# Graph network, three projections: the next tile's rows turned ahead of this tile's products, and the v's turned one tile later

## The chip, the cores and the metric

The kernel runs on one core of a Trainium2 chip. The metric is the device time of one execution in microseconds (us), the median of several runs. Engines are called by their names in the profile: PE is TensorE (matrix products and transposes; PEld is its loading of weights), DVE is VectorE, ACT is ScalarE, POOL is GpSimd, and SP is the engine that issues most transfers.

## The reference, cut to what matters

A graph of 2708 nodes with 512 features passes four layers, each of the form x = layernorm(x + layer(x, adj)). The first two average neighbours; the third is graph attention with 8 heads of 64; the fourth is graph attention with 8 heads, a second attention with one head of 512, and a small MLP. The change lies in the projections of the attentions:

```python
Wh = jnp.einsum('ni,hio->hno', h, W)              # the projection
f1 = jnp.einsum('hno,ho->hn', Wh, a1)             # per target row
f2 = jnp.einsum('hno,ho->hn', Wh, a2)             # per source row
e = leaky_relu(f1[:, :, None] + f2[:, None, :], 0.2)
attention = softmax(where(adj > 0, e, -9e15), axis=-1)
h_prime = jnp.einsum('hnm,hmo->hno', attention, Wh)
```

The projection is made three times: for layer 2 (8 heads), for the first attention of layer 3 (8 heads), and for its second attention (one head; called the output layer here). Between the last two an elu is applied.

## The kernel before, in words

The 2708 rows are cut into 22 tiles, 21 of 128 rows and one of 20. `project` (L502) makes one projection; it is called at L892 for layers 2 and 3 and at L897 for the output layer. For each tile t it does the following.

- The rows of the tile come from DRAM. `source` says how: `plain` (L758) only loads them; `summed` (L761) loads the attention's output `rows` and the old features `spare`, adds them (L764), normalises (`layer_norm`, L106: bn_stats L108, L110, L112, a power on POOL L113, L114) and stores the result to `x3_dram` (L766); `elu_first` (L769) loads and applies an elu (L753 to L756, its exponential on ACT). The tile `rows` has three buffers, `spare` two.
- `transposed` (L116) turns the rows: four transposes on PE into the PSUM tile `ps_tr` (L120), then one copy on ACT to `xT` (L122). Both have two buffers. The helper `early` (L145) makes results once and some tiles ahead: the rows one tile ahead of the turning (L521), the turned rows when they are asked for (L522).
- Eight products (L529) accumulate over four slices of 128 features into two PSUM tiles, `pm0` and `pm1`, of two buffers each: 256 columns of Wh each, and behind them the columns for f1 (in `pm0`) or f2 (in `pm1`). The profile counts each product twice, as two passes.
- From `pm`, DVE copies the f2 part to `dcol` (L534) and the clamped f1 part to `b` (L536, two buffers). ACT makes exponentials of them (`ecol` L538, `ucol` L539, `vcol` L549), and Wh is scaled into `R2` (on DVE, L543, with heads; on ACT, L547, without). The profile writes `R` for R2.
- `b` is turned on PE into `ps_v` (L556), and ACT writes its exponential into a row of `vrow` (L557). Where a block of target tiles is complete, `vrow` is sent to `v_dram` (L560). There are two blocks of 11 tiles in layers 2 and 3, and six of up to 4 tiles in the output layer. At the end of a block in layers 2 and 3, DVE also splits factors into bf16 parts (L563 to L568, `split` L493).

The attention follows. Each head and block loads its row of `v_dram` over all partitions (`v_bc`, L592). For each source tile, DVE makes the weights `e` (L598, four buffers), ACT a mask `c` of them by a sigmoid (L606), and PE multiplies `e` with R2 (L734). The output layer's attention multiplies at L857 and then runs the MLP (L823, L832).

What sets the order of the work: the program is written as one stream, and the framework's scheduler orders each engine's instructions from it by the dependences and by its own estimate of times. It may move an instruction before others that stand ahead of it in the source, so attention work of the first block (`e`, `c`) comes to stand among the later tiles of a projection. The order on each engine is then fixed, and each engine waits in it for the semaphores of the others. Transfers that SP issues (`rows`, `spare`, `v_dram`, `v_bc`) share one such queue. In the projection no order is written out by hand.

Of the kernel before, what the change touches and what calls it, by code (L numbers as in the profile page):

```python
# [9 lines left out]
F32 = mybir.dt.float32  # L10
# [3 lines left out]
AF = mybir.ActivationFunctionType  # L14
# [4 lines left out]
P = 128  # L19
# [3 lines left out]
ALPHA = 0.2  # L23
# [7 lines left out]
def kernel(  # L31
# [9 lines left out]
    nc = tc.nc  # L41
    N = x.shape[0]
    NT = -(-N // P)
    FULL = N // P
    H, HO = l2_w.shape[0], l2_w.shape[2]
# [4 lines left out]
    def rows(t):  # L50
        return min(P, N - t * P)
# [9 lines left out]
    ident = const.tile([P, P], F32, name="ident")  # L61
# [54 lines left out]
    def transposed(pool, psum, src, n, name, order=as_it_comes):  # L116

        ps = psum.tile([P, KD, P], F32, name="ps_tr")
        for k in range(KD):
            order(nc.tensor.transpose(ps[:, k, :n], src[:, k * P:(k + 1) * P], ident[:n, :n]))  # L120
        dst = pool.tile([P, KD, P], F32, name=name)
        nc.scalar.copy(dst[:, :, :n], ps[:, :, :n])  # L122
        return dst
# [15 lines left out]
    def weight_tile():  # L139
        return ahead.tile([P, KD, 2, D // 2 + H], F32, name="w", bufs=1)  # L140
# [4 lines left out]
    def early(first, n, make):  # L145

        made = {}

        def get(i, **how):
            for j in range(len(made), min(i + first + 1, n)):  # L150
                made[j] = make(j, **how)
            return made[i]
        return get
# [36 lines left out]
    with ExitStack() as phase:  # L190
# [16 lines left out]
        sm = phase.enter_context(tc.tile_pool(name="l01", bufs=2))  # L207
# [19 lines left out]
        with ExitStack() as ph:  # L227
# [36 lines left out]
            xTs = early(0, NT, lambda t, order=as_it_comes: transposed(ahead, ps_tr, xs(t), rows(t), "xT", order))  # L264
# [11 lines left out]
            for t in range(NT):  # L276
                n = rows(t)
# [25 lines left out]
        with ExitStack() as ph:  # L303
            st = ph.enter_context(tc.tile_pool(name="l0b", bufs=1))
            b_nb = bias(bcast(l0_b_nb, D))
            cuts = [(b, min(b + 4, NT)) for b in range(0, NT, 4)]
            cuts = cuts[-1:] + cuts[:-1]
# [87 lines left out]
            for i, b in enumerate(cuts):  # L395
                ts_ = range(*b)
                cols, w = slice(b[0] * P, b[1] * P), (b[1] - b[0]) * P
# [17 lines left out]
                for t in ts_:  # L415
                    n = rows(t)
# [8 lines left out]
            xTs = early(0, NT, lambda t: transposed(ahead, ps_tr, xs(t), rows(t), "xT"))  # L425
            for t in range(NT):
                n = rows(t)
# [9 lines left out]
        with ExitStack() as ph:  # L437
            st = ph.enter_context(tc.tile_pool(name="l1b", bufs=2))
            for t in range(NT):
                n = rows(t)  # L440
# [52 lines left out]
    def split(pool, dst, src):  # L493

        rest = pool.tile([P, NT, H], F32, name="rest", bufs=1)[:, :src.shape[1], :src.shape[2]]
        nc.vector.tensor_copy(dst[:, :, :, 0], src)
        nc.vector.tensor_sub(rest, src, dst[:, :, :, 0])
        nc.vector.tensor_copy(dst[:, :, :, 1], rest)
        nc.vector.tensor_sub(rest, rest, dst[:, :, :, 1])
        nc.vector.tensor_copy(dst[:, :, :, 2], rest)  # L500

    def project(name, source, layer, v_dram, cuts):  # L502


        w_src, w_view, _, heads = atts[layer]

        w = weight_tile()
        hh = max(heads // 2, 1)
        for k in range(KD):
            for a in range(2):  # L510
                src = (w_src[4 * a:4 * a + 4, k * P:(k + 1) * P, :].rearrange("h p o -> p h o") if heads > 1 else
                       w_src[k * P:(k + 1) * P, a * D // 2:(a + 1) * D // 2].rearrange("p (h o) -> p h o", h=1))
                nc.scalar.dma_start(w[:, k, a, :D // 2].rearrange("p (h o) -> p h o", h=hh), src)
        nc.gpsimd.tensor_copy(w[:, :, :, D // 2:D // 2 + heads], wa[:, layer, :, :, :heads])
        with ExitStack() as ph:
            sm = ph.enter_context(tc.tile_pool(name=f"{name}_s", bufs=2))
            ps_tr = ph.enter_context(tc.tile_pool(name=f"{name}_ptr", bufs=2, space=PSUM))
            ps_mm = ph.enter_context(tc.tile_pool(name=f"{name}_pmm", bufs=2, space=PSUM))
            ps_v = ph.enter_context(tc.tile_pool(name=f"{name}_pv", bufs=2, space=PSUM))
            width = max(z - a for a, z in cuts) * P  # L520
            xs = early(1, NT, lambda t: source(sm, t, rows(t)))  # L521
            xTs = early(0, NT, lambda t: transposed(ahead, ps_tr, xs(t), rows(t), "xT"))  # L522
            for t in range(NT):
                n = rows(t)
                xT = xTs(t)
                pm = [ps_mm.tile([P, D // 2 + H], F32, name=f"pm{a}") for a in range(2)]
                for k in range(KD):
                    for a in range(2):
                        nc.tensor.matmul(pm[a][:n, :D // 2 + heads], xT[:, k, :n], w[:, k, a, :D // 2 + heads],  # L529
                                         start=(k == 0), stop=(k == KD - 1))  # L530
                if t + 1 < NT:
                    xTs(t + 1)
                d = dcol[:n, t, :heads]
                nc.vector.tensor_copy(d, pm[1][:n, D // 2:D // 2 + heads])  # L534
                b = sm.tile([P, H], F32, name="b")
                nc.vector.tensor_scalar(b[:n, :heads], pm[0][:n, D // 2:D // 2 + heads], -RANGE, RANGE,  # L536
                                        op0=OP.max, op1=OP.min)
                nc.scalar.activation(ecol[:n, t, :heads], d, AF.Exp, scale=ALPHA)  # L538
                nc.scalar.activation(ucol[:n, t, :heads], d, AF.Exp, scale=1.0 - ALPHA)  # L539
                for a in range(2):  # L540
                    to, src = R2[:n, t, a * D // 2:(a + 1) * D // 2], pm[a][:n, :D // 2]
                    if heads > 1:
                        nc.vector.tensor_mul(to.rearrange("p (h o) -> p h o", h=hh),  # L543
                                             src.rearrange("p (h o) -> p h o", h=hh),
                                             ecol[:n, t, a * hh:(a + 1) * hh, None].to_broadcast([n, hh, HO]))
                    else:
                        nc.scalar.activation(to, src, AF.Copy, scale=ecol[:n, t, 0:1])  # L547
                if heads > 1:
                    nc.scalar.activation(vcol[:n, t, :], b[:n, :], AF.Exp, scale=ALPHA - 1.0)  # L549
                    nc.gpsimd.tensor_scalar(bcol[:n, t, :], ucol[:n, t, :], -STEP * (1.0 + 2.0 ** -22), None,  # L550
                                            op0=OP.mult)
                a, z = next(c for c in cuts if c[0] <= t < c[1])
                if t == a:
                    vrow = sm.tile([heads, width], F32, name="vrow", bufs=1)
                ps = ps_v.tile([P, P], F32, name="ps_v")
                nc.tensor.transpose(ps[:heads, :n], b[:n, :heads], ident[:n, :n])  # L556
                nc.scalar.activation(vrow[:, (t - a) * P:(t - a) * P + n], ps[:heads, :n], AF.Exp, scale=ALPHA - 1.0)  # L557
                if t == z - 1:
                    cols = slice(a * P, a * P + (z - 1 - a) * P + n)
                    nc.sync.dma_start(v_dram[:, cols], vrow[:, :cols.stop - cols.start])  # L560
                    if heads > 1:
                        ue = sm.tile([P, NT, H], F32, name="ue", bufs=1)[:, :z - a]
                        nc.vector.tensor_mul(ue, ucol[:, a:z], ecol[:, a:z])  # L563
                        split(sm, parts_m[:, a:z], ue)
                        for k in range(2):
                            nc.vector.tensor_scalar(pairs_c[:, a:z, :, k, 6 * k:6 * k + 3], parts_m[:, a:z, k::2, :],
                                                    -1.0, None, op0=OP.mult)
                            split(sm, pairs_c[:, a:z, :, k, 6 * k + 3:6 * k + 6], ecol[:, a:z, k::2])  # L568
            sq = sm.tile([P, NT, H], F32, name="sq", bufs=1)
            if heads < H:  # L570
                nc.vector.memset(sq, 0.0)
            dd = dcol[:, :, :heads]
            nc.vector.tensor_mul(sq[:, :, :heads], dd, dd)
            sq = sq.rearrange("p t h -> p (t h)")
            nc.vector.tensor_scalar(sq, sq, RANGE * RANGE, None, op0=OP.is_le, op1=OP.add,
                                    accum_out=okc[:, layer:layer + 1])
# [33 lines left out]
    cuts = [-((-NT * i) // nb) for i in range(nb + 1)]  # L610
# [278 lines left out]
    for i, (source, dst) in enumerate(((plain, o_dram[0]), (summed, o_dram[1]))):  # L889
        with ExitStack() as ph:  # L890
            att = Weights(ph, f"a{2 + i}", blocks, vd[i])
            project(f"p{2 + i}", source, i, vd[i], blocks)  # L892
            heads_attention(f"a{2 + i}", att, dst)
# [332 lines left out]
```

## Time and profile before

The time is 3125.3 us, the median of three runs (3123.17 to 3129.33). The profiled execution has a span of 3125.8 us at a mean granted TensorE clock of 0.996.

| Stretch (us from the span's start) | What runs there | PE busy | DVE busy | ACT busy |
|---|---|---|---|---|
| 925 to 1024 | projection of layer 2 | 92.84 of 99 | 35.91 | 40.63 |
| 1609 to 1718 | projection of layer 3 | 96.98 of 109 | 72.05 | 38.58 |
| 2305 to 2404 | projection of the output layer | 92.74 of 99 | 37.96 | 48.71 |
| all, 3125.8 | | 3009.5 | 1988.8 | 1401.3 |

How to read it: a stretch is a part of the one execution on the chip that the profile shows. Busy times count the instructions of an engine; matrix products are pipelined, so that a busy PE need not be at its peak. In a line of the timeline stand start, duration, engine, line of the source, operation, the tiles written and read, and in square brackets how long the engine was idle before and what it waited for. The projections take about a tenth of the span.

### The profile page before, as it was taken

The page shows a single profiled execution, that of the slowest core. Times are in us where ns is not written, and L with a number is a line of the kernel's source. Part 1 is how long each engine was busy: PE and PEld are TensorE (multiplying, and loading weights), DVE is VectorE, ACT ScalarE, POOL GpSimd, SP SyncE. Part 2 cuts the span into 40 slices and gives each one's busy share as a digit, 9 for nine tenths or more (in the row PEclk, how much of TensorE's full clock was granted, in tenths as well). Part 3 has the DMA queues.
Part 4 walks back from the last instruction along what each step waited for, and adds up shares of the span by engine and source line. Part 5 has one row for each costly group of instructions (what it writes and reads, how often), then busy time and mean ns, then how long its engine had stood idle before and what let it go on. Part 6 is the DMA issues. An engine that isn't in the chain of part 4 may idle for free.

```text
span 3125.8 us, 37086 instructions
## 1 busy us (share of the span) xinstructions
PE 3009.5 (96%) x14888; PEld 1647.0 (53%) x14888; DVE 1988.8 (64%) x2562; ACT 1401.3 (45%) x1575; POOL 223.2 (7%) x352
## 2 busy tenths in 40 slices
PE   8999999999999999999998999999999999999998
PEld 4556666448887433333356333333356455555555
DVE  5562765212233899999986999999963524345342
ACT  2431000112224688888863788899863000000011
POOL 2220010101110000000012000000000000000001
PEclk9999999999999999999999999999999999999999
DMA  5651421322222000110024010011021000000000
GB/s 137 139 127 35 121 64 41 108 65 81 81 70 76 15 29 35 39 44 30 28 80 145 22 39 28 27 38 33 20 97 48 4 14 17 24 14 22 14 19 21
DMA packets 114287, 163.31 MB, mean 52 GB/s; under 512 B 39494, under 2 KB 62311, under 8 KB 114104
## 3 DMA queue, kind: packets, MB, share of 16 engines
q1 hardware_dynamic: 88152, 109.21, 11.5%
q0 software_dynamic: 16064, 47.95, 5.6%
q10 hardware_dynamic: 9888, 3.67, 0.5%
q8 instruction: 119, 1.95, 0.3%
q14 instruction: 64, 0.52, 0.1%
HBM read 130.92 MB, written 44.55 MB: 56 GB/s over the span
## 4 chain that ended last, share of the span: by engine, by line
PE 65%; issue 19%; DVE 10%; ACT 2%; DMA 2%; POOL 1%; DVEq 0%; POOLq 0%; SPq 0%; ACTq 0%
PE pn L857 13%; PE pm L221 10%; PE po L734 9%; PE acc L450 7%; DVE e L598 6%; PE acc L408 5%; PE pm L529 5%; PE pl L832 5%; PE pl L823 5%; PE pd L665 2%; ACT c L606 1%; PE ps_tr L120 1%; PE acc L254 1%; DMA rows<-o_dram 1%; PE pm L401 1%
## 5 line engine op out<-in xcount | busy, mean ns | idle before, releaser
L598 DVE SCALAR_TENSOR_TENSOR e<-v_bc,ucol,maskT 128x1300 f32<-128x1300 f32 (+3 forms) x836 | 1187.4, 1473 | 345.6 <-PE pn L857 317.9
L606 ACT ACTIVATE c<-e,bcol 128x1300 fp8e4<-128x1300 f32 (+1 forms) x704 | 993.9, 1423 | 113.0 <-DVE e L598 61.7
L734 PE MATMUL po<-e,R 128*64 128x512 f32 (+2 forms) x4224 | 946.4, 550 | 47.4 <-DVE e L598 47.3
L734 PEld LDWEIGHTS po<-e,R 128*64 128x64 f32 x4224 | 340.5, 136 | 600.3 <-issue 384.9
L857 PE MATMUL pn<-e,R 128*128 128x512 f32 (+1 forms) x1056 | 413.5, 542 | 0.0
L857 PEld LDWEIGHTS pn<-e,R 128*128 128x128 f32 x1056 | 191.0, 190 | 199.4 <-issue 195.9
L529 PE MATMUL pm<-w,xT 128*128 128x264 f32 (+3 forms) x1056 | 247.7, 388 | 17.1 <-ACT xT L122 16.6
L529 PEld LDWEIGHTS pm<-w,xT 128*128 128x128 f32 (+1 forms) x1056 | 191.3, 187 | 58.5 <-ACT xT L122 24.4
L408 PE MATMUL acc<-yH,kT 128*128 128x512 f32 x484 | 214.0, 442 | 0.0
L825 ACT ACTIVATE w<-pl,b 128x256 f32<-128x256 f32 (+1 forms) x88 | 40.9, 465 | 372.9 <-PE pl L823 372.9
L450 PE MATMUL acc<-yH,mf 128*128 128x512 f32 x484 | 192.7, 398 | 0.0
L408 PE MATMUL acc<-yL,kT 128*128 128x512 f32 x484 | 192.4, 398 | 0.0
L450 PE MATMUL acc<-yL,mf 128*128 128x512 f32 x484 | 190.2, 393 | 0.0
L221 PE MATMUL pm<-w,xT 128*128 128x512 f32 (+1 forms) x384 | 175.1, 598 | 2.4 <-ACT xT L122 1.4
L113 POOL TENSOR_TENSOR ln_rs<-ln_rs,half 128x1 f32<-128x1 f32 x88 | 51.6, 586 | 1693.0 <-DVE ln_rs L112 1691.7
L221 PE MATMUL pm<-weight,xT 128*128 128x512 f32 (+1 forms) x352 | 162.3, 604 | 3.6 <-DVE weight L133 2.8
L313 DVE SCALAR_TENSOR_TENSOR kT<-pm,maskT 128x512 fp32r<-128x512 f32 (+1 forms) x132 | 84.8, 642 | 123.6 <-PE pm L311 122.9
L832 PE MATMUL pl<-lin,w 128*128 128x512 f32 (+1 forms) x352 | 157.4, 592 | 0.0
L823 PE MATMUL pl<-lin 128*128 128x256 f32 (+1 forms) x704 | 153.4, 371 | 3.7 <-DVE lin L756 3.7
L823 PEld LDWEIGHTS pl<-lin 128*128 128x128 f32 x704 | 129.1, 190 | 34.5 <-issue 15.8
L447 ACT CAST mf<-maskT 128x1024 fp32r<-128x1024 fp8e4 (+1 forms) x66 | 64.3, 976 | 163.2 <-PE acc L450 160.9
L215 ACT CAST yH<-pm 128x512 fp32r<-128x512 f32 (+1 forms) x44 | 25.7, 585 | 245.7 <-PE pm L221 245.7
(172 smaller groups left out, 2518.3 us busy)
## 6 DMA issues: line engine op xcount, KB each, us to landing
rows<-x_dram SPq DMA_DIRECT2D x63, 256.0 KB
m<-in_adj_dram POOLq DMA_DIRECT2D x21, 677.0 KB, 6.3
v_bc<-v_dram SPq DMA_DIRECT2D x16, 704.0 KB
x_dram<-u POOLq DMA_DIRECT2D x42, 256.0 KB, 2.3
rows<-o_dram SPq DMA_DIRECT2D x42, 256.0 KB
v_bc<-v_dram SPq DMA_DIRECT2D x16, 650.0 KB
o_dram<-o SPq DMA_DIRECT2D x32, 256.0 KB
rows<-in_x_dram SPq DMA_DIRECT2D x21, 256.0 KB
```

What stands on the lines that cost most here:

```text
L221: order(nc.tensor.matmul(pm[:n], xT[:, k, :n], w[:, k, :], start=(k == 0), stop=(k == KD - 1)))
L313: nc.vector.scalar_tensor_tensor(kT[:, :w], cum[:, :w], KEEP, maskT[:, j, cols], op0=OP.is_le, op1=OP.mult)
L408: nc.tensor.matmul(pa[t], kT[:, (t - b[0]) * P:(t - b[0] + 1) * P], y[:, j, :], start=(j == 0 and y is yH), stop=(j == NT - 1 and y is yL))
L447: nc.scalar.copy(mf[:, :g1 - g0, :], maskT[:, g0:g1, t * P:(t + 1) * P])
L450: nc.tensor.matmul(pa, mf[:, j - g0, :], y[:, j, :], start=(j == 0 and y is yH), stop=(j == NT - 1 and y is yL))
L529: nc.tensor.matmul(pm[a][:n, :D // 2 + heads], xT[:, k, :n], w[:, k, a, :D // 2 + heads], start=(k == 0), stop=(k == KD - 1))
L598: nc.vector.scalar_tensor_tensor(e[:, :w], v[:, :w], ucol[:, j, h:h + 1], maskT[:, j, c0:c0 + w], op0=OP.max, op1=OP.mult)
L606: nc.scalar.activation(c[:, :w], e[:, :w], AF.Sigmoid, bias=bcol[:, j, h:h + 1], scale=STEP, saturate=False)
L734: pe(nc.tensor.matmul(po[i][HO * k:HO * k + HO, :c1 - c0], R2[:, j, h * HO:(h + 1) * HO], e[:, c0:c1], start=(j == 0), stop=(j == NT - 1)))
L823: nc.tensor.matmul(pl[:, :w], self.lin1[:, k, f * P:(f + 1) * P], h[:, k, :w], start=(k == 0), stop=(k == KD - 1))
L832: nc.tensor.matmul(pl[:n], gT[:, f, (t - t0) * P:(t - t0) * P + n], self.lin2[:, f, :], start=(f == 0), stop=(f == KF - 1))
L857: nc.tensor.matmul(pn[k][:, :w], R2[:, j, k * P:(k + 1) * P], e[:, :w], start=(j == 0), stop=(j == NT - 1))
```

## The change

In the loop over the tiles, the rows of tile t+1 are turned before the products of tile t are issued, not after them. And `b` of tile t is turned after the products of tile t+1, by a function `keep_v` that is called one tile later; the row of v's and its transfer go with it, and after the loop the last tile's is done. The purpose is that PE always has something to do while the other engines work: the copy of the turned rows to `xT` gets the time of a whole tile's products, and the transpose of `b` no longer stands right behind the products that `b` comes from. The splits at the end of a block stay where they were. No instruction is added or taken away.

```diff
             xTs = early(0, NT, lambda t: transposed(ahead, ps_tr, xs(t), rows(t), "xT"))
+            vrows, bs = {}, {}
+
+            def keep_v(t):
+                n = rows(t)
+                a, z = next(c for c in cuts if c[0] <= t < c[1])
+                if t == a:
+                    vrows[a] = sm.tile([heads, width], F32, name="vrow", bufs=1)
+                vrow = vrows[a]
+                ps = ps_v.tile([P, P], F32, name="ps_v")
+                nc.tensor.transpose(ps[:heads, :n], bs[t][:n, :heads], ident[:n, :n])
+                nc.scalar.activation(vrow[:, (t - a) * P:(t - a) * P + n], ps[:heads, :n], AF.Exp, scale=ALPHA - 1.0)
+                if t == z - 1:
+                    cols = slice(a * P, a * P + (z - 1 - a) * P + n)
+                    nc.sync.dma_start(v_dram[:, cols], vrow[:, :cols.stop - cols.start])
+
             for t in range(NT):
                 n = rows(t)
+
                 xT = xTs(t)
+                if t + 1 < NT:
+                    xTs(t + 1)
                 pm = [ps_mm.tile([P, D // 2 + H], F32, name=f"pm{a}") for a in range(2)]
...
-                if t + 1 < NT:
-                    xTs(t + 1)
+                if t:
+                    keep_v(t - 1)
                 d = dcol[:n, t, :heads]
                 nc.vector.tensor_copy(d, pm[1][:n, D // 2:D // 2 + heads])
-                b = sm.tile([P, H], F32, name="b")
+                b = bs[t] = sm.tile([P, H], F32, name="b")
...
-                if t == a:
-                    vrow = sm.tile([heads, width], F32, name="vrow", bufs=1)
-                ps = ps_v.tile([P, P], F32, name="ps_v")
-                nc.tensor.transpose(ps[:heads, :n], b[:n, :heads], ident[:n, :n])
-                nc.scalar.activation(vrow[:, (t - a) * P:(t - a) * P + n], ps[:heads, :n], AF.Exp, scale=ALPHA - 1.0)
                 if t == z - 1:
-                    cols = slice(a * P, a * P + (z - 1 - a) * P + n)
-                    nc.sync.dma_start(v_dram[:, cols], vrow[:, :cols.stop - cols.start])
                     if heads > 1:
...
+            keep_v(NT - 1)
             sq = sm.tile([P, NT, H], F32, name="sq", bufs=1)
```

## The prediction

> **What bounds the kernel now.** I read the page first (shares and groups), then the waits of TensorE in the three stretches of the projections, then the timeline of TensorE there, and last the timelines of ScalarE, VectorE and the transfer queue around each gap.
>
> ```profile
> PE 3009.5 (96%) x14888; PEld 1647.0 (53%) x14888; DVE 1988.8 (64%) x2562; ACT 1401.3 (45%) x1575; POOL 223.2 (7%) x352
> L529 PE MATMUL pm<-w,xT 128*128 128x264 f32 (+3 forms) x1056 | 247.7, 388 | 17.1 <-ACT xT L122 16.6
> L529 PEld LDWEIGHTS pm<-w,xT 128*128 128x128 f32 (+1 forms) x1056 | 191.3, 187 | 58.5 <-ACT xT L122 24.4
> ```
>
> TensorE is the engine in use all along; the group that the change touches waits 17 us, nearly all for `xT`, the copy of the turned rows. Each product is two passes, so a tile is 16 rows of this group. The projections lie at 925 to 1024 (layer 2), 1609 to 1718 (layer 3) and 2305 to 2404 us (output layer). In them the waits of TensorE for `xT`, `b` and `rows` sum to 5.5, 11.5 and 5.5 us. One pair of tiles of layer 2, on TensorE:
>
> ```profile
> 960.16 3.83 PE L529 MATMUL pm<-w,xT 128*128 128x264 f32 x16 [0.18 <-ACT xT L122]
> 963.82 0.27 PE L556 MATMUL ps_v<-ident,b 128*8 128x128 f32 x1
> 963.93 3.73 PE L529 MATMUL pm<-w,xT 128*128 128x264 f32 x16
> 967.49 0.60 PE L120 MATMUL ps_tr<-ident,rows 128*128 128x128 f32 x4
> 967.93 0.27 PE L556 MATMUL ps_v<-ident,b 128*8 128x128 f32 x1
> 968.04 0.60 PE L120 MATMUL ps_tr<-ident,rows 128*128 128x128 f32 x4
> 968.82 3.83 PE L529 MATMUL pm<-w,xT 128*128 128x264 f32 x16 [0.18 <-ACT xT L122]
> ```
>
> Both tiles' rows are turned in one lump, and the next product stands right behind, waiting for the copy. A pair takes 968.82 - 960.16 = 8.66 us. Without a break it would be two products of 3.57 (967.49 - 963.93), two turned v's of 0.11 and two turned row tiles of 0.44: 8.24 us. So 0.42 us a pair is lost: 0.18 of wait, the rest the refill after it.
>
> Around tile 12 the wait grows, because ScalarE puts the attention's first `c` and two table loads ahead of the copy:
>
> ```profile
> 985.02 1.28 ACT L606 ACT_TABLE_LOAD   x1 [2.35 <-DVE e L598]
> 986.32 1.47 ACT L606 ACTIVATE c<-e,bcol 128x1408 fp8e4<-128x1408 f32 x1
> 987.70 0.56 ACT L122 COPY xT<-ps_tr 128x512 f32<-128x512 f32 x1
> 988.31 3.83 PE L529 MATMUL pm<-w,xT 128*128 128x264 f32 x16 [1.59 <-ACT xT L122]
> ```
>
> Layer 3 also has to add, normalise and store each row tile, with three `rows` buffers, and runs at 9.5 us a pair:
>
> ```profile
> 1652.85 1.73 SPq L160 DMA_DIRECT2D rows<-o_dram  x2
> 1655.78 0.69 DVE L764 TENSOR_TENSOR rows<-rows,spare 128x512 f32<-128x512 f32 x1 [1.13 <-DMA rows<-o_dram]
> 1656.50 2.61 SPq L160 DMA_DIRECT2D spare<-x_dram  x2
> 1658.07 0.69 DVE L764 TENSOR_TENSOR rows<-rows,spare 128x512 f32<-128x512 f32 x1 [0.87 <-DMA rows<-o_dram]
> ```
>
> VectorE waits for the loads inside its in-order queue, and the next loads wait behind the next `spare` for VectorE: a ring. What follows each projection (attention, then MLP) starts from its last tile.
>
> **What the Trainium skill says.** PSUM — Partial Sum Buffer, Engine vs sequencer instructions: matmuls start in program order, and the queues of the other engines are strict first-in first-out. The trace agrees: the copy at 987.70 sits behind the `c`, and TensorE runs nothing else meanwhile. Perfetto Trace Analysis, Optimization Strategy: a gap that repeats on the busy engine can mean too few buffers for the next tile; here the 0.18 us gap repeats, but the cause is the order, since `xT` and `ps_tr` have two buffers and need no third. DMA: Bandwidth & Descriptors, Anatomy of one DMA: about 2.0 us plus bytes over 436 GB/s, an estimate of 2.6 us for 256 KB; in this trace 2.93 us pass from the issue to the use (1655.78 - 1652.85).
>
> **The change part by part.** The counts of instructions are the same; only places move. The order of the built programs shows it: before, `product(t), v(t-1), product(t+1), rows(t+2), v(t), rows(t+3)`; after, evenly `product(t), v(t-1), rows(t+2), product(t+1)`.
>
> Rows ahead: the copy for t+2 now runs beside product t+1 (3.57 us against 0.56). Its buffer was freed by product t. Nothing on TensorE waits for it in the steady state: 0.42 us a pair go.
>
> v's later: `ps_v` is read a tile after `b`, so its wait for VectorE goes. `b` keeps two buffers, which is enough, as v(t) stands before b(t+2). New: the row of v's for the first block leaves a tile later, and `v_bc`, the first four `e` and their `c` with it. Queued behind a waiting `e` are VectorE's copies out of `pm`, for which product t+2 waits; that slack is about 2.5 us.
>
> Layer 2. Tiles 0 to 11 and 17 to 21 run at 4.12 each. In between I follow the new order with durations from the trace: v row out at 975.4 (973.2 before), `e` from 984; `R(13)` stands behind three `e` of 1.6, so product 15 waits about 2.3 us. ScalarE now has three switches to sigmoid and back there, not four (1.28 each way). End: 925.5 + 21 x 4.12 + 3.7 + 2.3 = 1018, against 1023.5. Gain 5.3; from 3 (a second such wait) to 7.4 (none).
>
> Layer 3. Start as before, 0.8 us sooner (product 2 at 1619.6). The queue's order is now `rows(k), spare(k+2), rows(k+1), spare(k+3)`, and `spare(k+1)`, ahead of `rows(k)`, waits for the add of k-1. So a tile takes at least add 0.69, issue 0.35, load 2.75 to 3.7 (both are in this stage; I take 3.3, as two loads now start together), 0.1 to wake: 4.4 us, ends 3.9 and 4.85. The slack of VectorE swallows the 0.3 over 4.12 for eight tiles or so. Product 11 then starts at 1657.5, against 1664.25: 6.7 won. From there to the end before took 53.5 us, with 45 the least. The splits (18 operations of some 0.2, VectorE nearly full at 3.4 a tile), the wait for `v_bc`, four `e` and now four sigmoid switches where there were three keep it: product 15 at 1682.5 and the end at 1711.7 by the same walk, 54 us, so nothing more is won. Gain 6, from 2 to 11.
>
> Output layer. A pair takes 8.78 (2347.87 - 2339.09) and needs 2 x 3.47 + 1.1 = 8.04: 0.74 a pair. But at the start `dcol(2)` now stands in VectorE's queue ahead of the elu of rows 3, so that elu waits for product 2, and rows 3 and 4 both stand ahead of product 3: it starts at 2322.8, not 2321.2, 1.6 lost. Then 18 tiles at 4.02 and the last 3.5: 2398.7, against 2403.4. Gain 4.7, from 3 to 7.
>
> Passed on: the attention after each projection is rigid (in layers 2 and 3 VectorE makes `e` at 1.6 us each, without breaks; at the end TensorE is full), and all it needs from the projection comes from its last tile; the last v row goes out a little later but is read only for the second block, over 200 us on. So gains pass one to one. Sum 5.3 + 6 + 4.7 = 16.0: 3125.3 - 16 = 3109.
>
> **Rivals.** (1) Full relief: every wait and refill goes, 7.4 + 11 + 7 or more, 23 to 27 us: 3098 to 3102. For it: the steady waits are all of one kind. Against: the adds, `e` and `c` that cause the long ones are still there. (2) Layer 3's ring of loads takes over from the wait for `xT`, at 4.8 us a tile, and the later v row costs what the order wins there: only 8 to 10 us are left, 3115 to 3117. For it: VectorE already waits 10 us there for `rows`. Against: today's ring has two loads and a store in 9.5 us, with the adds of two tiles bunched. (3) No change: the attention's VectorE work absorbs what TensorE gains, 3120 to 3130. Against: its first four `e` are ready before the projection ends, and the next waits for TensorE. (4) Slower: the later `v_bc` holds VectorE's queue so long that the products stall by 5 us and more in both layers, and the gains are eaten: 3132. Against: half of the pairs lie before any `e`, and the output layer has none of this weight.
>
> **How the numbers follow.** Forecast (gain 11 to 22) 0.58, full relief 0.14, ring 0.18, no change 0.06, slower 0.04. Faster by over 0.2% (6.3 us) is the first three: 0.90. The range holds the forecast and most of the ring and stops just at full relief: 3102 to 3117.
>
> **What would show it.** Right: in layer 2 nearly no TensorE wait for `xT` before tile 13 and starts 4.12 us apart; one wait of about 2 us at product 15, for `R`; `b` no more a releaser of `ps_v`; layer 3's early products under 4.5 us apart, its VectorE waits for `rows` still there; product 3 of the output layer later than 2321 less what was won before it, then 4.02 a tile. Wrong: projection stretches as long as before, or attention stretches longer by what the projections won.

## The result, and the profile after

The changed kernel takes 3101.0 us, the median of four runs (3099.7 to 3101.4), against 3124.6 for the kernel before in the same session (3123.2 to 3129.3): a ratio of 0.9921, 95% interval 0.9904 to 0.9938. A second session gave 3101.1 against 3127.4, ratio 0.9916 (0.9902 to 0.9930). So the change is worth 23.7 us (26.3 by the second session), not the 16.0 of the forecast. From the page after, the engine's total and the group of the products:

```profile
PE 3000.0 (97%) x14888; PEld 1646.8 (53%) x14888; DVE 1988.2 (64%) x2562; ACT 1401.4 (45%) x1575; POOL 224.9 (7%) x352
L547 PE MATMUL pm<-w,xT 128*128 128x264 f32 (+3 forms) x1056 | 246.4, 387 | 3.7 <-DVE R L561 3.4
L547 PEld LDWEIGHTS pm<-w,xT 128*128 128x128 f32 (+1 forms) x1056 | 192.1, 187 | 39.1 <-DVE R L561 3.4
```

The instructions are the same; the busy time of TensorE falls by 9.5 us, 6.6 of it in the three projections and 2.5 ahead of them. The idle time ahead of the products falls from 17.1 to 3.7 us, and no product waits for `xT` any more. (L529 is now L547, `ps_v` L556 is L532, `b` L536 is L554, `dcol` L534 is L552, `R` L543 and L547 are L561 and L565, `e` L598 is L610.) In layer 2 the timeline of TensorE is even:

```profile
959.89 3.73 PE L547 MATMUL pm<-w,xT 128*128 128x264 f32 x16
963.46 0.27 PE L532 MATMUL ps_v<-ident,b 128*8 128x128 f32 x1
963.57 0.60 PE L120 MATMUL ps_tr<-ident,rows 128*128 128x128 f32 x4
964.00 3.73 PE L547 MATMUL pm<-w,xT 128*128 128x264 f32 x16
```

One product, one turned v, one turned row tile, 4.11 us, with nothing in between, where a pair of tiles took 8.66.

To see where the time went, the execution is cut at three places that both programs have: the first product of layer 2, the first turned `oT` ahead of layer 3's first product, and the same ahead of the output layer's (`oT` is the attention's output, turned back on TensorE at its end); the last piece ends at the first `pn`, where the output layer's attention begins. Each piece is a projection with the attention behind it (in the output layer, the projection alone).

| Stage (us, by the timeline of TensorE) | before | after | won | forecast |
|---|---|---|---|---|
| ahead of layer 2 (unchanged code) | 925.47 | 922.96 | 2.51 | 0 |
| layer 2 | 683.60 | 677.06 | 6.54 | 5.3 |
| layer 3 | 696.29 | 686.89 | 9.40 | 6 |
| output layer | 99.35 | 91.65 | 7.70 | 4.7 |
| behind it (unchanged code) | 721.09 | 721.04 | 0.05 | 0 |

The first row is no gain of the change: 2.4 us of it are there by 20 to 23 us, most of it in one product at 12 us that takes 5.61 us in the one profile and 3.70 in the other, and the other runs below start layer 2 anywhere from 922.1 to 925.1. The three stages sum to 23.64, close to the 23.67 of the medians. Each column is one profiled execution, and the old order varies from one to the next, as the runs below show; so the gains of single stages are good only to 3 to 5 us in layers 2 and 3, and to 1 us in the output layer.

### The profile page after: what moved, and what is told of

The parts are those of the page before. It is cut to its first block, busy times and chain, and to the rows that moved or that the text cites. A ratio compares the mean times of both kernels' runs of the same rounds, so it can differ in the third digit from the quotient of the medians.

```text
span 3099.6 us, 37155 instructions
## 1 busy us (share of the span) xinstructions
PE 3000.0 (97%) x14888; PEld 1646.8 (53%) x14888; DVE 1988.2 (64%) x2562; ACT 1401.4 (45%) x1575; POOL 224.9 (7%) x352
## 3 DMA queue, kind: packets, MB, share of 16 engines
q10 hardware_dynamic: 9888, 3.67, 0.5%
## 4 chain that ended last, share of the span: by engine, by line
PE 67%; issue 19%; DVE 9%; DMA 2%; ACT 2%; POOL 1%; SPq 0%; DVEq 0%; POOLq 0%; ACTq 0%
PE pn L869 13%; PE pm L221 10%; PE po L746 9%; PE acc L450 7%; PE pm L547 6%; DVE e L610 6%; PE acc L408 5%; PE pl L844 5%; PE pl L835 5%; PE pd L677 2%; PE ps_tr L120 1%; ACT c L618 1%; PE acc L254 1%; DMA rows<-o_dram 1%; PE pm L401 1%
## 5 line engine op out<-in xcount | busy, mean ns | idle before, releaser
L610 DVE SCALAR_TENSOR_TENSOR e<-v_bc,ucol,maskT 128x1300 f32<-128x1300 f32 (+3 forms) x836 | 1189.2, 1476 | 342.3 <-PE pn L869 316.5
L547 PE MATMUL pm<-w,xT 128*128 128x264 f32 (+3 forms) x1056 | 246.4, 387 | 3.7 <-DVE R L561 3.4
L547 PEld LDWEIGHTS pm<-w,xT 128*128 128x128 f32 (+1 forms) x1056 | 192.1, 187 | 39.1 <-DVE R L561 3.4
```

Of the source, the lines that this page charges most:

```text
L610: nc.vector.scalar_tensor_tensor(e[:, :w], v[:, :w], ucol[:, j, h:h + 1], maskT[:, j, c0:c0 + w], op0=OP.max, op1=OP.mult)
```

## The experiments

All fourteen, in one table; the stages are cut as above. Edits are to the changed kernel, except in e7.

| Run | Edit | Median | layer 2 | layer 3 | output |
|---|---|---|---|---|---|
| e1 | rows ahead alone | 3112.4 | 678.14 | 691.93 | 96.21 |
| e9 | v's later alone | 3126.6 | 682.36 | 702.01 | 97.34 |
| e2 | change in layer 2 alone | 3116.2 | 677.23 | 693.93 | 98.68 |
| e3 | change in layer 3 alone | 3119.1 | 686.80 | 687.00 | 99.07 |
| e4 | change in the output layer alone | 3122.1 | 686.50 | 699.05 | 91.65 |
| e5 | three pairs of `pm` | 3103.5 | 678.60 | 685.07 | 92.72 |
| e12 | the same, not in layer 2 | 3104.4 | 678.16 | 687.27 | 92.70 |
| e6 | `e` behind the projection, layers 2, 3 | 3103.5 | 680.78 | 683.80 | 91.65 |
| e13 | the same in layer 3 alone | 3098.6 | 677.23 | 684.00 | 91.64 |
| e10 | layer 3 as e6, output as e5 | 3099.0 | 677.38 | 684.55 | 92.71 |
| e11 | e10, `b` and `sq` off `o`'s place | 3100.0 | 677.40 | 684.07 | 92.59 |
| e7 | before, `b` off `o`'s place | 3127.3 | 686.01 | 694.83 | 98.29 |
| e8 | `b` off `o`'s place | 3100.7 | 677.05 | 686.83 | 91.38 |
| e14 | none | 3101.1 | 677.36 | 686.80 | 91.65 |

The kernel before took 3126.9 to 3128.1 in these sessions. Read down a column: the changed order, where a run has it unaltered, gives nearly the same stage whatever stands in the others: layer 3 686.80 to 687.00, the output layer 91.64 to 91.65, layer 2 677.06 to 677.38, but for e12, where it takes 678.16 with the same code (the 1.1 us come bit by bit in its attention). So a difference of 1 us in a single stage of a single run proves nothing. The old order varies more: layer 2 takes 683.60, 686.80, 686.50 and 686.01, layer 3 696.29, 693.93, 699.05 and 694.83, the output layer 99.35, 98.68, 99.07 and, in e7, 98.29.

**Each stage alone (e2, e3, e4).** The edit makes the two moves depend on the layer (here for layer 2, in short; the call of `keep_v` behind the loop depends on it too):

```diff
-                if t + 1 < NT:
+                if t + 1 < NT and layer == 0:
                     xTs(t + 1)
...
-                if t:
+                if t + 1 < NT and layer != 0:
+                    xTs(t + 1)
+                if t and layer == 0:
                     keep_v(t - 1)
...
+                if layer != 0:
+                    keep_v(t)
```

> The change in layer 2's projection alone, the other two in the old order. Theory A, three separate reliefs as the two traces show them (layer 2 6.5, layer 3 9.4, output layer 7.7 us): 6.5 less than before, 3118; from first product to layer 3's first turned row 6.5 us shorter than before. Rival B, the sizes of the forecast (5.3, 6, 4.7) are right and some 7 us came from elsewhere in the program: 5.3 less. Rival C, a gain of one stage is partly given back in the attention behind it: under 4 us less.

> The change in layer 3's projection alone. Theory A: 9.4 us less than before, 3115; products 3 to 14 start 4.12 us apart, paced by TensorE, not by the ring of loads (4.4). Rival B: 6 us less, 3119, and it is the relief of layer 2 that lets layer 3 run better in the full change. In both the first 1609 us are as before.

> The change in the output layer's projection alone. Theory A: 7.7 us less than before, 3117; product 3 starts about 14.5 us after the first turned o of the stage, against 15.9 before, then 4.02 us a tile. Rival B, the start of the stage loses 1.6 us as forecast and the gain in the full change came through layer 3: 4.7 us less, 3120, product 3 at 17.4 us.

The medians are 11.9, 9.0 and 5.9 us below before, each by some 4 us uncertain; the ratios are 0.9964 (0.9952 to 0.9977), 0.9972 (0.9960 to 0.9983) and 0.9976 (0.9965 to 0.9988). The stages are the finer measure: 677.23, 687.00 and 91.65, each as in the full change; in e4 product 3 starts at 14.56 us. The three gains, 0.36, 0.28 and 0.24%, sum to 0.88, and the whole change has 0.84 in e14: within the noise, the stages are separate. So theory A of all three holds for the stage that was changed; the totals of e3 and e4 agree with it, that of e2 is larger than its 6.5 us. There layer 3, in the old order, took 2.4 us less than in the profile of before, which is within its own variation; that no stage helps another at all is therefore not shown to better than that. Nothing is handed back in the attention.

**Each half alone (e1, e9).**

```diff
-                if t:
-                    keep_v(t - 1)
...
                 a, z = next(c for c in cuts if c[0] <= t < c[1])
+                keep_v(t)
...
-            keep_v(NT - 1)
```

> Only the rows are turned ahead; the v's stay in their own tile. (In the built programs each half of the change alone gives the very same order: two products, rows, v, rows, v, and again; so this run stands for either half.) Theory A, the two halves only work together: the rows are still turned in twos right in front of the product that needs their copy, so the 0.2 to 1.1 us wait for xT per pair stays; 3118 to 3126 us, and TensorE waits for xT over 12 us in L547's group. Rival B, the rows ahead are the gain and the v's only tidy up: 3101 to 3108 us, wait for xT under 6 us.

Neither theory holds, and the sentence in brackets is wrong: the order of e1 is even in the trace, while that of e9 is in twos, so one run could not stand for both. e1 gains 15.7 us (ratio 0.9948, 0.9931 to 0.9964), some six tenths of the whole change's. No product waits for `xT`, as B says. But the turned v now stands right behind the products that its `b` comes from. The waits of TensorE in layer 3 of e1 (in all, times, longest, us):

```profile
PE ps_v L532 <- DVE b L556: 6.3, 11, 1.2
```

In layer 2 VectorE is in time for it, and e1's stage is only 1.1 longer than with both halves; in layer 3, where VectorE also normalises, it is 5.0 longer, and in the output layer 4.6. The other half:

```diff
-                if t + 1 < NT:
-                    xTs(t + 1)
...
+                if t + 1 < NT:
+                    xTs(t + 1)
                 if t:
                     keep_v(t - 1)
```

> The other half: the v's turned one tile later, the rows at their old place. The built order is two products, rows, v, rows, v. Theory A, in this order the copy of xT (0.56 us) lies beside v, rows, v (0.11 + 0.44 + 0.11 = 0.66), so the 0.18 to 0.19 us waits for xT of a pair go even though the rows are not ahead; layer 2's stage is 678 to 681 us (old order 683.6 to 686.8 in four runs, full change 677.1), layer 3's 691 to 695 (old 694 to 699, full 686.9), the output layer's 96 to 98 (old 98.3 to 99.4, full 91.65): 3112 to 3120. Rival B, the v's matter only for ps_v's waits: all stages within 1 us of the old order's, 3123 to 3128. Rival C, two products back to back wait for VectorE to empty pm: slower than before in layer 3.

By itself it is worth nothing: ratio 1.0000 (0.9992 to 1.0009). The theory was right on the mechanism in layer 2's early tiles, and wrong on the rest. The timeline of TensorE there:

```profile
955.64 0.60 PE L120 MATMUL ps_tr<-ident,rows 128*128 128x128 f32 x4
956.08 0.27 PE L532 MATMUL ps_v<-ident,b 128*8 128x128 f32 x1
956.19 0.60 PE L120 MATMUL ps_tr<-ident,rows 128*128 128x128 f32 x4
956.63 0.27 PE L532 MATMUL ps_v<-ident,b 128*8 128x128 f32 x1
956.97 7.39 PE L547 MATMUL pm<-w,xT 128*128 128x264 f32 x32
```

The second v covers most of the copy of `xT`, so the wait is gone from the brackets; but two products run back to back, the rows come in a lump, and a pair of tiles still takes 8.56 us, against 8.66 before and 8.22 with both halves. In layer 3 a v then waits 4.34 us for `b`, which stands on VectorE behind an add that waits for its rows and behind an `e`, and `xT` is waited for 5.8 us in all; that stage is 702.01, the longest of any run. So the whole is where rival B has it, and layer 3 is slower as in rival C, but not for its reason: no product there waits for VectorE. For the whole gain both halves are needed: the rows ahead to make the order even, the v's later to take `b` off it.

**What is left at tiles 13 to 19 (e5, e6, e13).** Two theories for it: too few `pm`, or the first `e` and `c` in the queues.

```diff
-            ps_tr = ph.enter_context(tc.tile_pool(name=f"{name}_ptr", bufs=2, space=PSUM))
-            ps_mm = ph.enter_context(tc.tile_pool(name=f"{name}_pmm", bufs=2, space=PSUM))
-            ps_v = ph.enter_context(tc.tile_pool(name=f"{name}_pv", bufs=2, space=PSUM))
+            ps_tr = ph.enter_context(tc.tile_pool(name=f"{name}_ptr", bufs=1, space=PSUM))
+            ps_mm = ph.enter_context(tc.tile_pool(name=f"{name}_pmm", bufs=3, space=PSUM))
+            ps_v = ph.enter_context(tc.tile_pool(name=f"{name}_pv", bufs=1, space=PSUM))
```

> The changed kernel with [...]three pairs of pm instead of two, and one ps_tr and one ps_v instead of two each. Theory A, what is left of the stalls at tiles 13 to 19 (1.1 us of waits in layer 2, 5.4 us in layer 3) is that product t+2 needs the pm of t, which VectorE empties late while it makes the first e's: a third pair gives it 4.1 us more, 1 us goes in layer 2 and 3 to 6 in layer 3: 3094 to 3098. Rival B, VectorE's own queue and the loads behind the v rows hold the later rows themselves, and a third pair only moves the wait from R to xT: 3099 to 3102. Rival C, one ps_tr and one ps_v cost more than that at the starts: over 3103.

The time is rival C's, by little: ratio 0.9926 (0.9912 to 0.9939), 2.4 us over the changed kernel's median. The two intervals overlap, and only 0.8 of the 2.4 lies in the three stages, so that a loss of the whole isn't shown. Layer 3 gains 1.8, but its tail only waits for something else (`ps_tr` 2.3 for the normalised rows, `ps_v` 1.2 for its one buffer), and the stages of layer 2 and the output layer get longer, the latter by 0.9 to 1.1 in each of the four runs with this edit (e5, e12, e10, e11). e12 keeps the third pair out of layer 2:

> The changed kernel with three pairs of pm (one ps_tr, one ps_v) in layer 3 and the output layer alone. Theory A, the stages are separate: layer 2 677.1 us as in the change, layer 3 685.1 and the output layer 90.5 as in the run with three pairs everywhere, so 2.9 less than the changed kernel: 3097 to 3099. Rival B, layer 3's 685.1 was luck of a stall that kept TensorE's clock: 686.5 to 689, 3099 to 3102.

Neither: 3104.4 us, ratio to before 0.9924 (0.9911 to 0.9938), and 3 us above the changed kernel's median. Layer 3's 687.27 is where rival B has it; why the same edit gave 685.07 in e5 stays open. The 90.5 us in this expectation, and in that of e10, was counted from the wrong group of turned `oT`; from the first one e5 takes 92.72. The start of layer 3 in e12 shows the cost that comes with each such stage, on TensorE:

```profile
1603.48 0.55 PE L698 MATMUL ps_t<-ident,oT 128*128 128x128 f32 x3 [0.61 <-DVE o L708]
1603.86 0.60 PE L120 MATMUL ps_tr<-ident,rows 128*128 128x128 f32 x4
1604.96 1.35 PE L547 MATMUL pm<-w,xT 128*128 128x264 f32 x5 [0.50 <-DVE o L708]
```

The first product now waits until VectorE has read the attention's last PSUM tiles; it starts 3.67 us after the first turned `oT`, against 1.31 in the changed kernel. e6 takes the `e` out instead, by one row of v's for all tiles, sent behind the last:

```diff
-            width = max(z - a for a, z in cuts) * P
+            width = NT * P if heads > 1 else max(z - a for a, z in cuts) * P
...
-                a, z = next(c for c in cuts if c[0] <= t < c[1])
+                a, z = (0, NT) if heads > 1 else next(c for c in cuts if c[0] <= t < c[1])
```

> The changed kernel with one row of v's for all tiles in layers 2 and 3, stored once, behind the last tile, so that no v_bc, e or c runs during these two projections. Theory A, the stalls of tiles 13 to 19 come from these: layer 2 goes through at 4.12 us a tile (end at 91 us from its first product at most), and in layer 3 product 11 to the end takes 45 to 48 us, not 52.8; the attention then starts without its first four e and behind the v_bc, 8 to 12 us later in each, so that the whole is slower, 3106 to 3116. Rival B, the stalls of layer 3 come from the splits and the normalisation: product 11 to the end stays over 50 us.

Theory A on the stalls: from product 11 to the last v, layer 3 takes 45.6 us instead of 53.0, with a single wait of 0.46. So the stalls do come from `v_bc`, `e` and `c`, taken together. Wrong was the price: the whole is 3103.5 (ratio 0.9925, 0.9910 to 0.9940), and layer 3's stage is even 3.1 shorter, while layer 2's is 3.7 longer. e13 makes the edit in layer 3 alone (`layer == 1` for `heads > 1`):

> The changed kernel with one v row for all tiles, stored behind the last, in layer 3 alone. Theory A, separate stages: layer 2 677.1 us, layer 3 683.8 to 684.6 (against 686.9), output layer 91.65; 2.3 to 3.1 us less than the changed kernel, 3097 to 3099. Rival B: the attention gives it all back and layer 3's stage is 686.5 or more; 3100 to 3102.

> The changed kernel, for comparison on the same chip: stages 677.1, 686.9 and 91.65 us, each within 0.3; 3100 to 3102 us. If the stages differ by more than 1 us from these, the differences between the other runs are within what the same program does by itself, and nothing follows from them.

Theory A: 3098.6 against 3101.1 on the same chip, ranges 3098.2 to 3100.1 and 3100.2 to 3103.3; it beats both kernels (ratio to before 0.9908, 0.9893 to 0.9923), and layer 3's stage is 2.3 to 3.1 shorter in all four runs with this edit (e6, e13, e10, e11). e14 repeats the stages of the changed kernel to 0.3 us, as expected. Layer 3's projection, from its first turned `oT` to the attention's first product (with `maskT`), is 96.04 long instead of 103.36, 7.3 won; the attention behind gives 4.4 back. VectorE there in e13, at the attention's start:

```profile
1701.70 1.69 DVE L610 SCALAR_TENSOR_TENSOR e<-v_bc,ucol,maskT 128x1408 f32<-128x1408 f32 x1 [2.33 <-DMA v_bc<-v_dram]
1703.30 0.25 DVE L671 COPY sums_m<-ps_t 128x96 f32<-128x96 f32 x1
1704.18 4.88 DVE L610 SCALAR_TENSOR_TENSOR e<-v_bc,ucol,maskT 128x1408 f32<-128x1408 f32 x3 [0.63 <-DMA v_bc<-v_dram]
```

and in the changed kernel:

```profile
1710.39 0.26 DVE L671 COPY sums_m<-ps_t 128x96 f32<-128x96 f32 x1 [3.60 <-PE ps_t L655]
1712.84 16.05 DVE L610 SCALAR_TENSOR_TENSOR e<-v_bc,ucol,maskT 128x1408 f32<-128x1408 f32 x10 [2.19 <-PE po L746]
```

With four `e` made early all their buffers are full, and VectorE stands idle for 3.60 and 2.19 us behind the projection; without them it uses that time. So the four early `e` (6.4 us of work), with their `v_bc` and `c`, save 4.4 us here, and cost 7.3 in the projection. In layer 2 they cost only 1.7 and save 5.4, which is why e6 loses there. Which of the three costs most was not tried apart.

**The mix, and the store of `o` (e10, e11, e7, e8).** e10 joins e13's edit with three pairs of `pm` in the output layer:

> The changed kernel with what helped single stages: layer 3 with one v row stored behind the last tile (its stage took 683.8 us, against 686.9), the output layer with three pairs of pm and one ps_tr and ps_v (90.5 against 91.65), layer 2 as in the change (677.1). Theory A, the stages are separate and add up: 3.1 + 1.1 less than the changed kernel, 3096 to 3098. Rival B, layer 3's gain hangs on what layer 2 did in that run: layer 3's stage back at 686 to 688, 3099 to 3101.

Neither: 3099.0 (ratio 0.9912, 0.9899 to 0.9926), where layer 3 gains 2.3 and the output layer loses 1.1. The last three ask whether VectorE's wait for the last store of `o`, 4.75 us at the start of the output layer before, set that start.

```diff
-                b = sm.tile([P, H], F32, name="b")
+                b = ahead.tile([P, H], F32, name="b")
```

> The kernel before, with the two buffers of b in a pool of their own place, not over the attention's o. Question: did the wait of b(0) for the last store of o (4.75 us at the output layer's start) set the start of that stage before, through v(0), which stands in front of product 2? Theory A: yes; b(0) no longer waits for the store, product 2 of the output layer starts at least 1 us sooner after the first turned o (10.9 before), and product 3 at 14.5 us or less (15.9 before); the same small gain in layer 3; 3120 to 3123. Rival B, the loads of rows set it: product 3 at 15.5 to 16 as before, 3124 to 3126.

> The same place for b in the changed kernel. Theory A, the change itself already took b(0) off the path, since product 2 goes ahead of v(0) and dcol(1) stands before b(0) for as long: within 0.5 us of the changed kernel at the start of the output layer, 3100 to 3102. Rival B: another 1 us or more there, 3097 to 3099.

```diff
-            sq = sm.tile([P, NT, H], F32, name="sq", bufs=1)
+            sq = sm.tile([P, NT, H], F32, name="sq", bufs=1) if heads > 1 else vcol[:, :NT]
```

> As the mix, and in the output layer neither b nor sq stand in memory where the attention's o was (sq takes over vcol, which is idle there). Theory A, VectorE's queue stood behind the store of o through either of the two, and the elu of rows 2 to 4 behind that; with both gone product 3 of the output layer starts 1 us or more sooner after the first turned o than in the mix: stage 89 to 89.8 us. Rival B, the loads of these rows, issued behind that store, set it: stage within 0.3 us of the mix's.

In e7 the wait only passed to the next tile in that place, as VectorE's timeline shows:

```profile
2315.83 0.20 DVE L571 MEMSET sq<- 128x176 f32 x1 [4.80 <-DMA o_dram<-o]
```

Still `b` was free, and product 3 of the output layer started at 15.05 us after the first turned `oT`, against 15.87 before (15.49 and 15.57 in e2 and e3): theory A in direction, half of it in size at most; the total shows nothing (ratio 1.0001, 0.9992 to 1.0009). On top of the change `b` alone is worth 0.27 in that stage (e8: theory A), and with `sq` 0.12 (e11 against e10: rival B). The change had already taken that wait off the path.

## Why the prediction was too small, point by point

Right, with the step as it was put:

- The bound and the mechanism: TensorE in order, the copy of `xT` behind a lump of rows. The steady loss per pair is gone in all three stages: 4.11 us a tile in layers 2 and 3, 4.02 in the output layer. Two small readings were off, without bearing on the sum: only one table load and the `c` stand ahead of the copy at 987.70 (the second load starts at 988.28, behind it), and of the 0.42 us a pair the 0.24 beside the wait are not all refill, since the transposes in front of it end 0.16 later than they would in a closed row (0.60, not 0.44).
- "`R(13)` stands behind three `e`", a wait at product 15 for `R`, and three sigmoid switches: all there. VectorE at the first `e` of layer 2, and in the second fence TensorE behind it:

```profile
979.75 1.68 DVE L610 SCALAR_TENSOR_TENSOR e<-v_bc,ucol,maskT 128x1408 f32<-128x1408 f32 x1
...
981.43 1.68 DVE L610 SCALAR_TENSOR_TENSOR e<-v_bc,ucol,maskT 128x1408 f32<-128x1408 f32 x1
...
984.35 1.68 DVE L610 SCALAR_TENSOR_TENSOR e<-v_bc,ucol,maskT 128x1408 f32<-128x1408 f32 x1
985.95 1.41 DVE L561 TENSOR_TENSOR R<-pm,ecol 128x256 f32<-128x256 f32 x4
```

```profile
986.42 7.39 PE L547 MATMUL pm<-w,xT 128*128 128x264 f32 x32 [1.08 <-DVE R L561]
```

- "Gains pass one to one": the table of stages and e2 to e4. It holds for this change, in which the same four `e` are ready when the projection ends; e6 and e13 show that it isn't a rule.

Where it failed, by the terms of the sum, 16.0 against 23.64:

1. Output layer, "1.6 lost" at the start: 1.3 was won, 2.9 of the 7.6 that are missing. The step names no new start for product 2, behind which it puts `dcol(2)` and the elu, so it seems to have kept the old one. But before, v(0) stood ahead of product 2 and waited 1.03 us for `b(0)`. TensorE before, up to product 2, and after:

```profile
2311.30 3.30 PE L529 MATMUL pm<-w,xT 128*128 128x257 f32 x14 [0.26 <-ACT xT L122]
2315.64 0.27 PE L556 MATMUL ps_v<-ident,b 128*1 128x128 f32 x1 [1.03 <-DVE b L536]
2315.74 0.60 PE L529 MATMUL pm<-w,xT 128*128 128x257 f32 x2
2316.18 0.27 PE L556 MATMUL ps_v<-ident,b 128*1 128x128 f32 x1
2316.29 3.63 PE L529 MATMUL pm<-w,xT 128*128 128x257 f32 x16
```

```profile
2292.53 4.93 PE L547 MATMUL pm<-w,xT 128*128 128x257 f32 x22
2297.30 0.27 PE L532 MATMUL ps_v<-ident,b 128*1 128x128 f32 x1
2297.41 2.33 PE L547 MATMUL pm<-w,xT 128*128 128x257 f32 x10
```

The 22 passes are product 1 and six of product 2: it starts at 2292.53 + 3.47 = 2296.0, 9.1 us after the first turned `oT` (2286.91), where it took 10.9; `dcol(2)` comes at 2298.04, and the elu behind it waits 0.93 us. Product 3 starts at 14.55, against 15.87 before and a forecast of 17.44. In e1, where the v's stay in their own tile, the built order puts them behind six passes of product 2 too, and products 2 and 3 start at 9.09 and 14.44: it is the rows ahead that move this start. All behind product 3 was right: 77.1 us to the first `pn`, where the forecast's terms and the 1.3 us to `pn` of before give 77.2.

2. Layer 3, "a tile takes at least 4.4 us" by the ring of loads, and 54 us from product 11 to the end: 9.40 was won, not 6. In parts, from the first turned `oT`: product 2 at 9.94, forecast 10.53 (0.6); products 2 to 11 in 37.08, not 37.9 (0.8); product 11 to the last v 53.0, not 54.2 by the forecast's times (1.2); attention 0.8. The ring never set the pace: the starts are 4.11 apart, and the adds wait for `rows` in four of eight tiles in the middle of the stretch, 3.6 us in all, and for TensorE in the other four. The load was mis-sized: the forecast took its 3.3 from times between issue and use; from issue to landing the trace after has, for the loads of these eight tiles,

```profile
DMA to landing us min/median/max: 2.4/2.4/3.1
```

With 2.4 the ring takes 3.5 us by the forecast's other terms. The tail was taken for as bad as before. It has other waits now (3.10 for `b`, 1.46 and 0.81 for `R`), a little shorter:

```profile
1666.74 0.37 PE L532 MATMUL ps_v<-ident,b 128*8 128x128 f32 x1 [3.10 <-DVE b L554]
1666.90 1.06 PE L120 MATMUL ps_tr<-ident,rows 128*128 128x128 f32 x4
1669.42 8.99 PE L547 MATMUL pm<-w,xT 128*128 128x264 f32 x32 [1.46 <-DVE R L561]
```

3. Layer 2, "product 15 waits about 2.3 us": 1.43 was lost there (products 14 to 17 take 13.76 us, and 3 x 4.11 is 12.33); the first `e` came 56.8 us after the first product, not 58.5. That and 0.4 of small terms turn the 5.3 into 6.54.

Of these three, only the output layer's miss is clear of the old order's own variation, which is 3 to 5 us in layers 2 and 3. So the likeliest case had its mechanism right and three terms too dear, each of them a loss by a new wait that was taken near its dear end; the time fell to the rival "full relief", by a way that is not quite that rival's, as losses of 1.4 us in layer 2 and some 7 in layer 3 remained.

## What to carry to other kernels

Before calling a new order of instructions a loss, see what the old order held at the same place: here v(0) had held product 2, so the new order started earlier than anything in the old trace. Two moves that each look like the whole remedy should be run apart: the rows ahead gave 15.7 us, the v's later nothing, both together 24 to 26. And work that is pulled ahead into a stage isn't free because its engine has gaps; whether it pays (layer 2) or not (layer 3) is seen in the engine's idle time behind the stage.

## What the runs showed of the hardware

A long wait of TensorE can cost more than its length. In e3, old order in layer 2, after waits of 1.04 and 2.50 us a product takes 6.42 us, against 3.73 elsewhere:

```profile
986.11 0.27 PE L532 MATMUL ps_v<-ident,b 128*8 128x128 f32 x1 [1.04 <-DVE b L556]
986.22 0.62 PE L120 MATMUL ps_tr<-ident,rows 128*128 128x128 f32 x4
989.33 6.42 PE L547 MATMUL pm<-w,xT 128*128 128x264 f32 x16 [2.50 <-ACT xT L122]
```

The granted clock from 989 to 996 us is 0.60 there. In e4 a wait of 2.50 us alone is followed by a product of 5.51 at 0.72. In layer 3 of the changed kernel the two products of 8.99 us above (7.39 without) lose 1.6 in the same way, at 0.82 from 1669 to 1679. In the profile of before, the waits of 1.59 and 1.77 are both followed by 3.83 at 1.00.

It isn't so every time. e7, at the same place as e3, after waits of nearly the same length:

```profile
986.60 0.27 PE L556 MATMUL ps_v<-ident,b 128*8 128x128 f32 x1 [0.87 <-DVE b L536]
986.71 0.62 PE L120 MATMUL ps_tr<-ident,rows 128*128 128x128 f32 x4
989.82 3.83 PE L529 MATMUL pm<-w,xT 128*128 128x264 f32 x16 [2.50 <-ACT xT L122]
```

The clock there is 1.00, and in e5 a wait of 2.57 us at 1703 to 1706 is followed by 1.00 too. So the length of a wait doesn't settle it; what does is not shown here. Nor does the clock explain why layer 2 in the old order takes 683.60 us in one profile and some 686 in others: e7 has 686.01 with no such product, e3 and e4 686.80 and 686.50 with one. The Trainium skill, TensorE: Matmul & The Clock Gate, What's actually happening, has the array's clock fall to half after an idle window of about 3.4 us; the traces agree in that the clock falls behind waits, though in e4 one of 2.50 us was enough.
